# Lists and router bias in bf16 terms, and tokens' weights stored in eight runs

## The chip, the cores and the metric

One NeuronCore of a Trainium2 chip runs the whole kernel. The metric is the device time of one execution in microseconds (us), taken as the median of several runs. Engines are named as in the profile: PE (TensorE, with its weight loads as PEld), DVE (VectorE), ACT (ScalarE), POOL (GpSimd) and SP (SyncE); SP, ACT and POOL also issue DMAs.

## The reference, cut to what matters

A graph layer is followed by a mixture of experts. 1024 nodes (tokens) have 512 features, there are 16384 edges sorted by destination, and 64 experts of which each token takes 2.

```python
HW = layernorm(x) @ W
x1 = x + relu(segment_sum(edge_val[:, None] * HW[edge_col], edge_row) + bias)
xt = layernorm(x1)
scores = sigmoid(xt @ Wg.T + bg)              # 1024 x 64
w, idx = top_k(scores, 2);  w = w / w.sum(-1, keepdims=True)
nx = layernorm(xt)
h1 = einsum('td,edh->eth', nx, gamma * W1) + b1 + beta @ W1
h3 = einsum('td,edh->eth', nx, gamma * W3) + b3 + beta @ W3
y  = einsum('eth,ehd->td', silu(h1) * h3 * cw, W2) + cw @ b2   # cw: w at the two chosen experts
z  = a small shared expert of 32 hidden units
out = x1 + y + z
```

The kernel computes each expert only for the tokens that chose it. All inputs and outputs are fp32.

## The kernel before, in words

P is 128. The 1024 tokens are NT = 8 tiles of 128 rows. The order of the work on each engine is written out by hand (`manual_schedule`): every engine runs its instructions in program order, and semaphores hold it where data is missing.

**Graph part.** The sorted edges are cut into 128 x 2 windows of destinations. For each of 16 groups `one_hots` builds selection matrices (DVE, ACT), `matrix_group` multiplies them on PE into a dense weighted adjacency, `turn` transposes it, and `weighted_sum` multiplies it with `hws`, the transformed features (tile `acc`, L514). In the second round of eight groups, at g = 6, `bias_terms` splits the experts' biases b1 and b3 into three bf16 terms each, whose sum gives the fp32 value; this splitting on DVE already exists before the change.

**Tile loop (L686).** Iteration t runs a pipeline over the tiles, whose steps share the engines:
- `weighted_sum` of tile t on PE, in three portions; between them stand `turn`, `listed(t - 3)`, `score_bias(t - 1)`, `turn_x(t - 1)`, `rank(t - 2)` and, last, `scores(t - 1)`.
- `finish(t)` on DVE: bias, relu, residual, statistics of the layer norm, normalized row (`res`, `bnst`, `mvr`, L529 to L541). `summed` loads the row's base from DRAM through POOL's queue.
- `store_nx(t - 1)`: ACT scales the row (L545), POOL stores it to `nx_d` in DRAM, from where experts' rows are gathered.
- `score_bias` (L558) opens the accumulation of the router's scores with a matmul of a row of ones with `brow`, the router's bias `bg` followed by zeros; `scores` (L563) adds the product with `wall`.
- `choose` (DVE) takes the best two experts; `rank` (PE, L597 and L599, bf16) counts how many earlier tokens chose the same expert; `put` (DVE) turns that into a slot (`here`, L611).
- `slots` (L614) builds two one-hot matrices for each of the two choices: `so` (L620), token by slot, and `bo` (L622), token by pair of experts, multiplied with the entry's number `numb`, 2 x token + choice - PAD with PAD = 16384. It runs on POOL, for the last tile on DVE. `listed` (L628) adds so^T bo into the PSUM tile `plist`, two fp32 matmuls for a tile. A profile shows each fp32 matmul of this kind as two instructions.

At the end `plist` plus PAD gives `lists` (L719), the entry numbers by pair of experts, 64 rows for each expert, and `tokens` (L720), half of them.

**Expert part (L1008).** 33 blocks are walked in `order`: 32 pairs of experts of up to 64 tokens each, and one block for experts with more than 64. For block n: `fetch` gathers token rows from `nx_d` (POOL, L752), `front` transposes and scales them (`scaled`: PE, DVE), `hidden` multiplies with W1 and W3 (L781) and applies Silu (ACT, L784), `turned` transposes (L793), `outputs` multiplies with W2 (L803) and copies to `xy` (ACT, L806), `scatter` writes the rows to `y_d` (POOL, L810). `load_until` has SP issue the expert weights, 512 KB a transfer, up to AHEAD = 13 experts ahead into a ring of tiles; a transfer waits until the tile's former reader on PE is done. `weights` (L826) divides the two best scores by their sum and stores them, 2048 numbers, to `w_d` in DRAM; it stands after the first block's `hidden`. The last blocks' weights are gathered from `w_d` by `block_weights`. `beyond`, at block 6, makes the lists for the experts with more than 64 tokens, with fp32 one-hot matrices of its own and `numb`. ACT fills the three gather buffers `rows_of` with zeros before the first gathers (L1010).

## Time and profile before

| what | value |
|---|---|
| median of 3 runs | 447.22 us (446.52 to 449.56) |
| the profiled execution's own time | 446.42 us |
| its span, first to last instruction | 444.7 us |
| PE / PEld busy | 391.5 us (88%) / 185.0 us (42%) |
| DVE / ACT / POOL busy | 243.8 / 117.2 / 122.0 us |
| DMA | 132.50 MB, mean 298 GB/s |
| mean granted TensorE clock | 0.966 |

Durations come from the one profiled execution. A busy PE is not PE at its peak, since matmuls are pipelined and their ends are modelled; the distance between two starts is the better measure of what an instruction holds PE for. The chain that ended last follows the last instruction back from releaser to releaser. A wait is put down to the semaphore that came last. In the timeline a matmul's bracket gives the idle time of the engine before it and what ended it. Names in the profile leave out buffer numbers: `ph<-brow,ones` is `score_bias`, `plist<-bo,so` is `listed`, `acc<-hw,AT` is `weighted_sum`, `pt<-ident,row` is `turn_x`, `pt<-ident,A` is `turn`.

### The profile page before, as it was taken

How to read it: one execution, taken by the hardware profiler on the slowest of the kernel's cores; microseconds unless marked ns; L12 is line 12 of the kernel's file. 1: busy time of each engine (PE TensorE's matmuls, PEld its weight loads, DVE VectorE, ACT ScalarE, POOL GpSimd, SP SyncE). 2: the span in 40 equal slices, each digit the busy share in tenths (PEclk: the TensorE clock that was granted, in tenths of full speed). 3: DMA queues.
4: the chain of work that ended last, by engine and by line, in shares of the span. 5: the costliest groups of instructions: out<-in, count | busy, mean ns of one | idle time of the engine just before them, and what ended most of it. 6: DMA issues, size and time to landing. Idle time of an engine off the chain costs nothing.

```text
span 444.7 us, 6426 instructions
## 1 busy us (share of the span) xinstructions
PE 391.5 (88%) x2130; PEld 185.0 (42%) x2130; DVE 243.8 (55%) x723; ACT 117.2 (26%) x241; POOL 122.0 (27%) x162
## 2 busy tenths in 40 slices
PE   2999769988999953799967999999999999999693
PEld 1554446644655542343422444343443443433141
DVE  4869899658777783423275444443424323421791
ACT  1235799332231130121101221212221221212100
POOL 5450800003333343223232232322322331303100
PEclk9999999999999975899998999999999999999898
DMA  8367392991723397379999999999999999998572
GB/s 255 105 109 107 127 359 104 408 370 67 255 70 127 123 407 285 134 248 412 409 407 407 407 409 405 409 408 408 406 408 407 409 407 406 406 407 343 193 298 89
DMA packets 40983, 132.50 MB, mean 298 GB/s; under 512 B 7116, under 2 KB 7260, under 8 KB 40816
## 3 DMA queue, kind: packets, MB, share of 16 engines
q1 hardware_dynamic: 31040, 109.66, 63.2%
q0 software_dynamic: 9184, 20.28, 14.9%
q10 hardware_dynamic: 720, 2.10, 1.2%
q8 instruction: 18, 0.29, 0.3%
q14 instruction: 21, 0.17, 0.1%
HBM read 124.13 MB, written 18.62 MB: 321 GB/s over the span
## 4 chain that ended last, share of the span: by engine, by line
PE 59%; DMA 13%; DVE 9%; ACT 5%; issue 2%; POOL 0%; POOLq 0%; ACTq 0%; DVEq 0%
PE xph L781 18%; PE acc L514 11%; DMA y_d<-xy,lists 10%; PE xpy L803 9%; PE xpt L193 3%; ACT ov L417 2%; PE ph L495 2%; PE xpht L793 2%; PE xph L777 2%; PE pt L507 1%; PE ph L563 1%; DMA y_d<-xy,lists_o 1%; PE xpy L942 1%; ACT A L500 1%; PE xpy L909 1%
## 5 line engine op out<-in xcount | busy, mean ns | idle before, releaser
L781 PE MATMUL xph<-w,xT 128*64 128x512 f32 (+1 forms) x520 | 122.5, 600 | 0.1
L810 POOL DMA_INDIRECT y_d<-xy,lists x30 | 31.1, 1037 | 145.3 <-ACT xy L806 53.7
L803 PE MATMUL xpy<-w,xhT 128*64 128x512 f32 (+1 forms) x260 | 66.0, 610 | 4.7 <-ACT xhT L795 4.7
L781 PEld LDWEIGHTS xph<-w,xT 128*64 128x64 f32 (+1 forms) x520 | 38.7, 139 | 62.2 <-issue 58.4
L786 DVE TENSOR_TENSOR xh<-xa,xph 128x256 f32<-128x256 f32 x33 | 13.9, 420 | 87.7 <-ACT xa L784 87.7
L514 PE MATMUL acc<-hw,AT 128*128 128x512 f32 x128 | 60.7, 600 | 0.4 <-ACT AT L508 0.4
L784 ACT ACTIVATE xa<-xph 128x256 f32<-128x256 f32 x33 | 12.6, 383 | 114.1 <-PE xph L781 114.1
L752 POOL DMA_INDIRECT rows<-nx_d,tokens x32 | 34.7, 1083 | 17.2 <-issue 7.3
L803 PEld LDWEIGHTS xpy<-w,xhT 128*64 128x64 f32 (+1 forms) x260 | 19.4, 141 | 45.0 <-issue 39.4
L764 DVE TENSOR_TENSOR xT<-xpt,gT 128x512 f32<-128x512 f32 x32 | 22.1, 689 | 26.5 <-PE xpt L193 26.2
L806 ACT COPY xy<-xpy 128x512 f32<-128x512 f32 x33 | 19.3, 585 | 49.8 <-PE xpy L803 44.1
L307 PE MATMUL ph<-w_sb,hT 128*128 128x512 f32 x64 | 31.2, 636 | 0.7 <-ACT hT L300 0.7
L514 PEld LDWEIGHTS acc<-hw,AT 128*128 128x128 f32 x128 | 22.1, 191 | 17.3 <-issue 16.7
L193 PE MATMUL xpt<-ident,rows 128*128 128x128 f32 x132 | 22.0, 293 | 5.9 <-DMA rows<-nx_d,tokens 5.9
L546 POOL DMA_DIRECT2D nx_d<-row x8 | 4.5, 560 | 73.8 <-ACT row L545 73.8
L417 ACT CAST ov<-eq 128x1536 f32<-128x1536 bf16 x16 | 24.7, 1552 | 0.0
L766 DVE TENSOR_TENSOR xT<-xT,bT 128x512 f32<-128x512 f32 x32 | 22.2, 693 | 1.1
L495 PE MATMUL ph<-ov,ol 128*32 128x128 f32 x512 | 17.4, 276 | 5.4 <-ACT A L500 5.0
L193 PEld LDWEIGHTS xpt<-ident,rows 128*128 128x128 f32 x132 | 19.3, 211 | 6.0 <-DMA rows<-nx_d,tokens 6.0
L793 PEld LDWEIGHTS xpht<-ident,xh 128*128 128x128 f32 x66 | 11.8, 212 | 20.8 <-DVE xh L786 12.7
L793 PE MATMUL xpht<-ident,xh 128*128 128x128 f32 x66 | 15.1, 311 | 6.0 <-DVE xh L786 6.0
L193 PE MATMUL pt<-ident,row 128*128 128x128 f32 x64 | 11.6, 306 | 8.4 <-DVE row L187 2.8
(271 smaller groups left out, 503.9 us busy)
## 6 DMA issues: line engine op xcount, KB each, us to landing
w<-in_L_ffn_W_dram SPq DMA_DIRECT2D x195, 512.0 KB, 11.1
y_d<-row POOLq DMA_DIRECT2D x1, 4096.0 KB, 14.5
ys<-y_d SPq DMA_DIRECT2D x8, 512.0 KB, 7.8
base_d<-in_L_gnn_bias_dram POOLq DMA_DIRECT2D x1, 2048.0 KB
row<-base_d POOLq DMA_DIRECT2D x8, 256.0 KB, 3.2
nx_d<-row POOLq DMA_DIRECT2D x8, 256.0 KB, 3.6
w_sb<-in_L_gnn_W_dram ACTq DMA_DIRECT2D x1, 1024.0 KB, 5.3
res<-in_x_dram SPq DMA_DIRECT2D x2, 512.0 KB, 10.6
```

The costliest lines, as they stand in the source:

```text
L193: nc.tensor.transpose(ps[:, k, :], v[:, k, :], ident[:n, :n])
L307: nc.tensor.matmul(ph, hT[:, k, :], w_sb[:, k, :], start=(k == 0), stop=(k == KC - 1))
L417: nc.scalar.copy(ov[:, :, :VA], eq)
L495: nc.tensor.matmul(pa[LO * w:LO * (w + 1), u, :], ol[:, q, :], ov[:, q, :], start=True, stop=True)
L514: nc.tensor.matmul(accs[t], ATs[h][t // 4][:, t % 4, wq, :], hws[h][:, wq, :], start=(h == 0 and wq == 0), stop=(h == NH - 1 and wq == NQ ...
L752: nc.gpsimd.indirect_dma_start(out=rows, out_offset=None, in_=nx_d[:, :], in_offset=bass.IndirectOffsetOnAxis(ap=of, axis=0), bounds_check ...
L764: nc.vector.tensor_tensor(xT.rearrange(view, n=n), pt.rearrange(view, n=n), g[:, :, :, None].to_broadcast(over), ALU.mult)
L766: nc.vector.tensor_tensor(xT.rearrange(view, n=n), xT.rearrange(view, n=n), b[:, :, :, None].to_broadcast(over), ALU.add)
L781: nc.tensor.matmul(ph[n * r:(n + 1) * r], xT[:, k, n * r:(n + 1) * r], w13[:, :, k, :], start=False, stop=(k == KC - 1))
L793: nc.tensor.transpose(pt[:, c, :], v[:, c, :], ident)
L803: nc.tensor.matmul(py[n * r:(n + 1) * r], hT[:, c, n * r:(n + 1) * r], w2[:, c, :], start=(c == 0), stop=(c == HC - 1))
L810: nc.gpsimd.indirect_dma_start(out=y_d[:, :], out_offset=bass.IndirectOffsetOnAxis(ap=numbers, axis=0), in_=y, in_offset=None, bounds_chec ...
```

## The change

- `slots` builds `so` and `bo` in bf16. Each entry number is split into two terms, the tile's base 256 t - 16384 and 2 x partition + choice (`near`, a new iota), so `bo` has two halves and one more instruction for each choice; `listed` adds four bf16 matmuls for a tile.
- `brow` becomes 65 rows, with `bg` loaded into rows 0, 32 and 64; at g = 6 a loop takes the three bf16 terms of the bias into those rows of `brow3`, and `score_bias` is one bf16 matmul with K = 65.
- `weights` transposes the two columns of weights on PE, copies them on ACT into an eight-row tile, and stores eight runs of 256 numbers.
- `weights` moves ahead of `front(0)`, behind the first three gathers.
- An activation with Silu on one column of `found` is added behind the filling of `rows_of`.

```diff
--- before.py
+++ after.py
@@ -230,6 +230,9 @@
             nc.gpsimd.iota(diff, pattern=[[1, P]], base=0, channel_multiplier=-1, allow_small_or_imprecise_dtypes=True)
             nc.gpsimd.iota(numb, pattern=[[2 * P, NT], [1, 2]], base=-PAD, channel_multiplier=2,
                            allow_small_or_imprecise_dtypes=True)
+
+            near = gp.tile([P, 2], F32, name="near")
+            nc.gpsimd.iota(near, pattern=[[1, 2]], base=0, channel_multiplier=2, allow_small_or_imprecise_dtypes=True)
             nc.gpsimd.iota(partid, pattern=[[0, 1]], base=0, channel_multiplier=1, allow_small_or_imprecise_dtypes=True)
             nc.gpsimd.iota(tile_at, pattern=[[P, NT]], base=0, channel_multiplier=0, allow_small_or_imprecise_dtypes=True)
             at_i = gp.tile([P, P], I32, name="at_i")
@@ -252,8 +255,12 @@
             nc.vector.tensor_scalar(win[:, 1:2], win[:, 0:1], float(P), None, op0=ALU.add)
             nc.vector.tensor_scalar(thr, win, float(DL), None, op0=ALU.mult)
             nc.vector.tensor_scalar(before_b, diff, 0.0, None, op0=ALU.is_gt)
-            brow = gp.tile([1, P], F32, name="brow")
+
+            BR = 65
+            brow = gp.tile([BR, P], F32, name="brow")
             nc.vector.memset(brow, 0.0)
+            brow3 = gp.tile([BR, P], BF16, name="brow3")
+            nc.vector.memset(brow3, 0.0)
 
 
 
@@ -343,7 +350,8 @@
             bs13 = gp.tile([1, 2 * HS], F32, name="bs13")
             nc.gpsimd.dma_start(bs13[:, :HS], bs1[None, :])
             nc.gpsimd.dma_start(bs13[:, HS:], bs3[None, :])
-            nc.gpsimd.dma_start(brow[:, :E], bg[None, :])
+            for n in range(3):
+                nc.gpsimd.dma_start(brow[32 * n:32 * n + 1, :E], bg[None, :])
             b13 = mid([3 * EH, 2, 2, H], "b13", F32)
             for n in range(3):
                 for a in range(2):
@@ -555,7 +563,7 @@
 
             def score_bias(t):
                 pls[t] = psh.tile([P, D], F32, name="ph")[:, :P]
-                nc.tensor.matmul(pls[t], ones[0:1, :], brow, start=True, stop=False)
+                nc.tensor.matmul(pls[t], ones_b[:BR, :], brow3, start=True, stop=False)
 
             def scores(t):
                 pl = pls.pop(t)
@@ -616,16 +624,20 @@
                 here = ohots.pop(t)
                 ohots[t] = []
                 for n in range(2):
-                    so = rt.tile([P, P], F32, name="so", bufs=4)
+                    so = rt.tile([P, P], BF16, name="so", bufs=4)
                     engine.tensor_scalar(so, rank_at, here[:, n:n + 1], None, op0=ALU.is_equal)
-                    bo = rt.tile([P, NP], F32, name="bo", bufs=4)
-                    engine.tensor_scalar(bo, iota[:, :NP], pair[:, t, n:n + 1], numb[:, t, n:n + 1],
+                    bo = rt.tile([P, 2, NP], BF16, name="bo", bufs=4)
+                    engine.tensor_scalar(bo[:, 0, :], iota[:, :NP], pair[:, t, n:n + 1], float(2 * P * t - PAD),
+                                         op0=ALU.is_equal, op1=ALU.mult)
+                    engine.tensor_scalar(bo[:, 1, :], iota[:, :NP], pair[:, t, n:n + 1], near[:, n:n + 1],
                                          op0=ALU.is_equal, op1=ALU.mult)
                     ohots[t].append((so, bo))
 
             def listed(t):
                 for n, (so, bo) in enumerate(ohots.pop(t)):
-                    nc.tensor.matmul(plist, so, bo, start=(t == 0 and n == 0), stop=(t == NT - 1 and n == 1))
+                    for m in range(2):
+                        nc.tensor.matmul(plist, so, bo[:, m, :], start=(t == 0 and n == 0 and m == 0),
+                                         stop=(t == NT - 1 and n == 1 and m == 1))
 
             As = [[big([P, P // NS, DL, HI // 2], "A") for n in range(2)]]
             for g in range(8):
@@ -659,6 +671,12 @@
                 matrix_group(As[1], 1, g, ohs.pop(0))
                 if g == 6:
                     bias_terms()
+                    for n in range(3):
+                        term = gp.tile([BR, P], BF16, name="term")
+                        nc.vector.tensor_copy(term, brow)
+                        nc.vector.tensor_copy(brow3[32 * n:32 * n + 1, :], term[32 * n:32 * n + 1, :])
+                        if n < 2:
+                            nc.vector.tensor_sub(brow, brow, term)
                 turn(As[0], 0, g)
                 if g:
                     n0, n1 = len(ahead) * (g - 1) // 7, len(ahead) * g // 7
@@ -828,7 +846,13 @@
         nc.vector.reciprocal(wts[:, :, 0], wts[:, :, 0])
         nc.vector.tensor_mul(wts[:, :, 1], top[:, :, 1], wts[:, :, 0])
         nc.vector.tensor_mul(wts[:, :, 0], top[:, :, 0], wts[:, :, 0])
-        nc.gpsimd.dma_start(w_d.rearrange("(i p n) o -> p i (n o)", p=P, n=2), wts)
+
+        pt = psx.tile([P, D], F32, name="xpy")
+        for n in range(2):
+            nc.tensor.transpose(pt[:NT, n * P:(n + 1) * P], wts[:, :, n], ident)
+        wT = bp.tile([P, D], F32, name="xy", bufs=2)[:NT, :2 * P].rearrange("i (p n) -> i p n", n=2)
+        nc.scalar.copy(wT.rearrange("i p n -> i n p"), pt[:NT, :2 * P].rearrange("i (n p) -> i n p", n=2))
+        nc.gpsimd.dma_start(w_d.rearrange("(i r) o -> i (r o)", i=NT), wT.rearrange("i p n -> i (p n)"))
 
         nc.vector.tensor_mul(rs2, vs[:, :, 0], rs[:, :, 0])
         nc.vector.tensor_mul(rs2, rs2, rs[:, :, 1])
@@ -1008,8 +1032,11 @@
     with tc.manual_schedule(engines={ENG.PE, ENG.DVE, ENG.Activation, ENG.Pool, ENG.SP}):
         for rows in rows_of:
             nc.scalar.activation(rows, ones[:, 0:1].to_broadcast([P, D]), AF.Copy, scale=0.0)
+
+        nc.scalar.activation(found[:, 0:1], ones[:, 0:1], AF.Silu)
         for n in range(NR):
             fetch(n)
+        weights()
         front(0)
         fetch(NR)
         front(1)
@@ -1040,8 +1067,6 @@
                 back(n - 1)
             else:
                 y_last = [outputs(*hTs.pop(LAST - 1))]
-            if n == 0:
-                weights()
             if n == BEYOND:
                 beyond()
             if 2 <= n - BEYOND < 2 + NT:
```

## The prediction

> **What bounds the kernel now.** I read the chain that ended last first, then the same chain in windows, then the timeline of each join, then the waits of SP's queue and the table of windows. The page's chain names the engines:
>
> ```profile
> PE 59%; DMA 13%; DVE 9%; ACT 5%; issue 2%; POOL 0%; POOLq 0%; ACTq 0%; DVEq 0%
> ```
>
> In order of time: up to 106 us DVE, ACT and PE alternate; from 106 to 155.6 us, the tile loop, every piece is PE's; to 178 us it is one long chain of small steps for the last tile, ending in the list and the first gather; from 178 us the experts run, PE's pieces to 346 us and then the scatters. One tile of the loop, in the chain (start, us, what):
>
> ```profile
> 107.95 3.44 PE acc L514 x8
> 111.39 0.45 PE pt L507 x4
> 111.83 0.37 PE plist L628 x4
> 112.20 1.80 PE acc L514 x4
> 114.00 0.41 PE ph L558 x2
> 114.41 0.68 PE pt L193 x4
> 115.09 0.03 PE ph L597
> 115.12 0.03 PE ph L599
> ```
>
> The reader is to see that the list (L628) and the router's bias (L558), both fp32, lie on PE's path in each tile, and that two bf16 matmuls of 64 columns (L597, L599) move it by 0.03 us each. A tile takes 9.88 us.
>
> **The experts.** Three resources are nearly level there. PE is busy 103.16 of 104 us between 241 and 345 us. SP's queue waits for room behind its own transfers (53.2, 47.8 and 46.8 us at L740, L734, L733 after 170 us) at 407 GB/s, and PE waits for a weight only at 401.7 us (0.7). Scatters wait for the one before from 350 us on. So a start that is earlier moves all three; a cheaper block in the middle would not.
>
> **The change, part by part.** Saved time is positive.
>
> *Bias, L558.* An fp32 matmul of K = 1 is two instructions; the new one is a single bf16 instruction of K = 65, 128 columns. The price is read from the starts: the four acc instructions before it start 0.43 apart from 112.03, so PE is free at 113.75, yet L558 starts at 113.93, and the transposes after it at 114.34. The bias thus takes 0.59 us of PE, of which its own columns explain 2 x 0.107 (as a 128-column fp32 transpose takes 0.107 in its group); the rest is gap on both sides. Lower bound of the new cost: twice L597's 64 columns, 0.06; upper: the same gaps remain and only one pass of columns goes, 0.43. I take 0.12, near the bf16 row, since the fp32 128-row matmuls show no such gaps. Saves 0.47 (0.16 to 0.53). On the path for tiles 2 to 6, five times: 2.35 (0.8 to 2.65). For tiles 0, 1 and 7 PE waits for DVE's row afterwards (2.1, 1.1 and 2.78 us idle): nothing.
>
> *List, L628.* Two fp32 matmuls (four instructions, 0.36 from start to start) become four bf16 instructions on twice the products. [...] The row: L597 and L599, with the same 128x128 bf16 weights, move PE by 0.03 each, so four cost 0.12 and a tile saves 0.24. [...] I take 0.20: saves 0.16 (-0.07 to 0.24), five times on the path: 0.8 (-0.35 to 1.2).
>
> PE reaches the rank (L597) 0.63 earlier per tile then. It now arrives 0.8 us after DVE's chosen (113.99 against 114.81), so 0.2 of cover is left; and DVE is idle 0.72 before each finish at 116.98. DVE is next in line but not yet late. If it is late by more, half of these 3.15 us stay.
>
> *Last tile.* Here the extra work lies on the path. Rank(7) stands on PE behind listed(6), which waits for POOL (timeline: start us, us, engine, line, operation, count, idle time before and its releaser):
>
> ```profile
> 165.78 0.47 POOL L622 TENSOR_SCALAR bo<-iota,pair,numb 128x32 f32<-128x32 f32 x1
> 166.30 0.50 PEld L628 LDWEIGHTS plist<-bo,so 128*128 128x128 f32 x2 [0.54 <-POOL bo L622]
> 166.75 0.24 PE L597 MATMUL ph<-chosen,before_b 128*128 128x64 bf16 x1
> 167.08 0.29 DVE L605 TENSOR_TENSOR tmp<-oh,ph 128x128 f32<-128x128 bf16 x1
> ```
>
> POOL gets two more bo instructions; bo to next so is 0.45 us, so it ends 0.9 later, and after it PE has one bf16 matmul instead of two fp32 instructions that took 0.45 here (166.30 to 166.75). Rank(7) is 0.6 later, and DVE's tmp, which has no slack (L592 ends as it starts), 0.57. Then DVE makes slots(7) itself, six instructions instead of four at 0.2 each: 0.4. Against it, after DVE's last bo only one short matmul follows instead of most of the four fp32 ones: from 169.16 to the lists at 169.92 are 0.76, then some 0.3. Sum: 0.57 + 0.4 - 0.46 = 0.5 lost (0 to 1.3; the upper end if each bo costs POOL 0.8, between its 0.47 and its slowest, 0.96). Earlier tiles have 2 us between POOL's last bo and listed, an iteration later, so 0.9 is covered; base loads, queued behind slots on POOL, are issued at 110.07 for use at 116.98 and land in 3.2: also covered.
>
> *Silu first.* At the first block ACT stands in PE's way:
>
> ```profile
> 184.02 1.28 ACT L784 ACT_TABLE_LOAD   x1 [17.43 <-PE xph L781]
> 185.31 0.38 ACT L784 ACTIVATE xa<-xph 128x256 f32<-128x256 f32 x1
> 186.21 0.50 PE L793 MATMUL xpht<-ident,xh 128*128 128x128 f32 x2 [2.26 <-DVE xh L786]
> 187.17 0.96 POOL L831 DMA_DIRECT2D w_d<-wts  x1 [7.68 <-DVE rs L834]
> ```
>
> PE waits 2.26 us through it. The added activation on one column pulls the load to about 167 us, into ACT's 17.43 idle us, with copies alone before the next Silu (copies between Silus load nothing now). Saves 1.28. [...] If Silu's set were dropped again, it saves 0.
>
> *Weights moved.* Six DVE instructions of 0.17 (1.1 us) now run from 170.3, two PE transposes (below 0.5) and an ACT copy (0.4) follow: done by about 172.7. All lie beside the first gather, issued at 171.22 on tokens that exist already and landing at 175.75. On POOL the store comes after three gathers, at 175.3, for 0.55 to 0.96, before fetch(3), which waits until 177.19 for PE's transposes. SP is passed nowhere. DVE's and ACT's queues hold nothing else until 176.96. Cost nothing; without that cover 2 us.
>
> *The store itself.* Before, 1024 pieces of 8 bytes; after, eight of 1 KB. This stands beside it now (window: us, busy PE, PEld, DVE, ACT, POOL, clock, DMA share, GB/s):
>
> ```profile
> 190.00:192.00 2.00, 2.00 (x12) 0.64 (x10) 0.42 (x1) 0.38 (x1) 0.00 (x0) 1.00 0.82 303
> 192.00:194.00 2.00, 2.00 (x14) 1.11 (x12) 0.36 (x1) 0.86 (x2) 0.32 (x1) 1.00 0.38 68
> 194.00:196.00 2.00, 2.00 (x12) 0.64 (x10) 1.02 (x2) 0.00 (x0) 1.69 (x2) 1.00 0.49 80
> 198.00:200.00 2.00, 2.00 (x14) 1.00 (x12) 0.28 (x1) 0.83 (x2) 0.00 (x0) 1.00 1.02 411
> ```
>
> Loads issued at 191 us hardly move for 4 us: about 3.3 us of the full rate are lost. Most of it should come back to DMA, which then no longer ends the last blocks; PE's two short waits near 401 and 408 us (0.7, 0.6) and a slow last scatter can shrink. As PE and the scatters are nearly as late, I count 0.3 (0 to 2).
>
> *Early parts.* One iota (0.14 to 0.22), larger memsets (0.17), two more bias loads on POOL (0.5 each, before POOL's 15.43 us wait at 44.10), and eight DVE instructions of some 0.2 at g = 6: DVE ends at 85.2 and is then idle 6.80 us until 92.01. Nothing; if that cover were gone, 1.8.
>
> **Sum.** 2.35 + 0.8 - 0.5 + 1.28 + 0.3 = 4.2 us. The profiled execution took 446.42 (span 444.7), giving 442.2. The median shown, 447.22, is 0.8 above it; I forecast 442.7 for a median, a little nearer to the profile because 449.56 pulls the three runs up.
>
> **Rivals.**
> [...]
> 2. *Experts pinned by DMA.* If the last weight rather than PE's start sets the end, the 1.28 is absorbed and only the loop's 2.65 remain: 444.5. For it: 407 GB/s throughout. Against: the lost 3.3 us come back to this very queue.
> 3. *DMA was the real bound.* Then the store's removal gives 2 us more: 440.5. Against: the scatters chain from 350 us.
> 4. *The loop turns to DVE, or the gaps around the bias remain.* About half of 3.15 stays: 444.3.
>
> **Numbers.** Forecast 0.44, rivals 0.09, 0.17, 0.14, 0.16. One per cent, about what a measurement of this kernel can tell, is 4.5 us, so the forecast lies on that line: half of it and rival 3 and a little more are faster (0.41), rivals 2 and 4 and the other half no change (0.50), rival 1 slower (0.09). The range, 439.8 to 446.8, takes in rivals 2 to 4 and the ends of the costs (bias -1.5, list -1.1, last tile -0.8).
>
> **To be seen after.** L558 one instruction, transposes at most 0.2 us after it starts; the tile pitch 9.25 instead of 9.88; POOL's last bo and rank(7) 0.6 later against here(6); no table load at the first L784; the dip of 68 to 80 GB/s gone. A pitch of 9.8, or a wait of listed for POOL in the loop, proves me wrong.

## The result and the profile after

The changed kernel takes 440.8 us (median of 4 runs, 440.67 to 442.39) beside 447.2 of the kernel before (four runs as well). The ratio is 0.988 (95% interval 0.984 to 0.993), which is 5.2 us less (3.4 to 7.1); the two medians differ by 6.4. The profiled execution took 440.67, its span is 438.9; before, 446.42 and 444.7.

The changed kernel's page, the chain that ended last by engine:

```profile
PE 62%; DMA 10%; DVE 9%; ACT 4%; issue 2%; POOL 0%; POOLq 0%; ACTq 0%; DVEq 0%
```

PE's share of the path has grown from 59% to 62% though its work shrank: what went was waiting on DMA and ACT. One tile of the loop in the changed kernel's chain (start, us, what). L522 was L514, L515 L507, L639 L628, L566 L558, L605 and L607 L597 and L599, L571 L563:

```profile
118.20 3.44 PE acc L522 x8
121.64 0.45 PE pt L515 x4
122.09 0.09 PE plist L639 x4
122.18 1.81 PE acc L522 x4
123.99 0.06 PE ph L566
124.05 0.53 PE pt L193 x4
124.58 0.03 PE ph L605
124.61 0.03 PE ph L607
```

The bias holds PE for 0.06 us, the list's four instructions for 0.09. The next tile starts at 127.32, so the pitch is 9.12 instead of 9.88, and there is still no wait for DVE or POOL in it.

Where ACT met the first block (timeline of the changed kernel: start, us, engine, line, operation; the bracket is idle time before and its releaser):

```profile
169.24 1.28 ACT L1036 ACT_TABLE_LOAD   x1
170.54 0.20 ACT L1036 ACTIVATE found<-ones 128x1 f32<-128x1 f32 x1
170.65 0.36 ACT L854 COPY xy<-xpy 8x256 f32<-8x256 f32 x1
180.33 0.38 ACT L802 ACTIVATE xa<-xph 128x256 f32<-128x256 f32 x1 [9.32 <-PE xph L799]
```

The load has gone into ACT's idle time, and L802 follows PE at once. The store's dip is gone as well (table of windows, changed kernel: window, us, busy PE, PEld, DVE, ACT, POOL, clock, DMA share, GB/s):

```profile
190.00:192.00 2.00, 2.00 (x12) 0.70 (x10) 0.07 (x1) 0.00 (x0) 1.01 (x1) 1.00 0.94 293
192.00:194.00 2.00, 2.00 (x10) 0.42 (x6) 0.42 (x1) 0.39 (x1) 0.00 (x0) 1.00 0.97 374
194.00:196.00 2.00, 2.00 (x14) 1.25 (x14) 0.91 (x2) 0.86 (x2) 0.00 (x0) 1.00 1.03 414
```

That much went as the forecast had it. To see the rest, I cut each trace at the same instructions: the first `acc` of tile 2, the first `acc` of tile 7, the `lists`, the first W1/W3 product of the second block, the ninth of the 16 W1/W3 products of the 31st block (its middle, 1.72 us behind its first in every trace), and the end of the span. The stretches in us, each from starts in the trace, with the experiments below beside them:

| kernel | to tile 2 | to tile 7 | to lists | to 2nd block | to mid-31st block | to the end | span |
|---|---|---|---|---|---|---|---|
| before | 91.81 | 55.08 | 23.03 | 17.44 | 208.82 | 48.48 | 444.7 |
| changed | 91.27 | 53.87 | 22.61 | 14.63 | 208.79 | 47.73 | 438.9 |
| e1 bias only | 91.48 | 54.73 | 22.84 | 14.39 | 208.84 | 45.00 | 437.3 |
| e2 lists only | 91.86 | 56.92 | 22.91 | 15.61 | 209.04 | 45.44 | 441.8 |
| e3 Silu only | 91.70 | 55.08 | 23.04 | 14.24 | 208.90 | 45.49 | 438.5 |
| e4 weights only | 90.80 | 56.74 | 23.31 | 14.39 | 208.82 | 46.74 | 440.8 |
| e5 changed again | 91.05 | 53.85 | 22.62 | 14.46 | 208.80 | 47.56 | 438.3 |
| e6 warm early | 91.61 | 52.20 | 22.62 | 15.86 | 207.21 | 46.75 | 436.2 |
| e9 tail's order | 91.95 | 55.09 | 22.65 | 14.92 | 208.81 | 45.34 | 438.8 |
| e10 warm and order | 90.96 | 52.21 | 23.09 | 13.87 | 209.99 | 43.91 | 434.0 |
| e12 changed, old store | 91.64 | 52.20 | 22.57 | 14.09 | 209.23 | 44.40 | 434.1 |

Each trace is one run. Those of e3 and e12 are of their fastest run (440.2 where the median is 444.1, 435.9 where it is 438.5), those of e2, e4 and e9 of their slowest. So the stretches tell where time goes, and the medians below how much.

Two things stand out in the first two rows. The stretch to tile 7 gained 1.21 us, though four pitches became shorter (three by 0.76, the last, which has no `turn`, by 0.58: 2.87 in all). And the first 91 us and the end gained 0.54 and 0.75 without an edit that explains it. The windows of the two kernels at tiles 2 and 3 say what happened, first the changed kernel's:

```profile
102.40:105.80 3.40, 1.33 (x8) 0.89 (x7) 2.99 (x18) 1.36 (x3) 0.54 (x1) 1.00 0.01 5
105.80:109.20 3.40, 3.40 (x11) 2.38 (x10) 2.98 (x9) 0.33 (x2) 2.13 (x4) 0.51 0.22 81
109.20:112.60 3.40, 3.40 (x11) 1.57 (x10) 2.91 (x18) 0.00 (x0) 1.63 (x4) 0.99 0.27 73
```

then the kernel before:

```profile
103.70:107.10 3.40, 1.89 (x9) 1.28 (x10) 3.05 (x18) 1.34 (x2) 0.54 (x1) 1.00 0.12 39
107.10:110.50 3.40, 3.40 (x15) 1.97 (x14) 3.13 (x12) 0.33 (x2) 3.00 (x5) 1.00 0.12 43
```

PEclk, the third figure from the right, is 0.51 in the changed kernel for one window after PE was busy 1.33 of 3.40 us, and 1.00 in the kernel before after 1.89 of 3.40. At half clock scores(0) and tile 3's first products took 1.66 us longer than before. In all traces the half-clock stretches, except the one that runs into a trace's end (5.1 us before, 4.0 in the changed kernel), are whole multiples of 3.41 us (3.4, 6.8, 17.1, 20.5), on a grid whose offset from the program's start differs from run to run (1.24 us before, 0.03 in the changed kernel).

### The profile page after: what moved, and what is told of

It is laid out like the page before. It is cut to its first block, busy times and chain, and to the rows that moved or that the text cites. A ratio compares the mean times of both kernels' runs of the same rounds, so it can differ in the third digit from the quotient of the medians.

```text
span 438.9 us, 6445 instructions
## 1 busy us (share of the span) xinstructions
PE 387.6 (88%) x2124; PEld 181.5 (41%) x2124; DVE 245.1 (56%) x734; ACT 117.8 (27%) x243; POOL 130.0 (30%) x179
## 4 chain that ended last, share of the span: by engine, by line
PE 62%; DMA 10%; DVE 9%; ACT 4%; issue 2%; POOL 0%; POOLq 0%; ACTq 0%; DVEq 0%
PE xph L799 20%; PE acc L522 12%; PE xpy L821 10%; DMA y_d<-xy,lists 7%; PE xpt L193 3%; ACT ov L425 2%; PE xpht L811 2%; PE xph L795 2%; PE ph L503 2%; PE ph L571 2%; PE pt L515 2%; PE xpy L966 1%; DMA y_d<-xy,lists_o 1%; ACT A L508 1%; PE xpy L933 1%
## 5 line engine op out<-in xcount | busy, mean ns | idle before, releaser
L799 PE MATMUL xph<-w,xT 128*64 128x512 f32 (+1 forms) x520 | 120.6, 599 | 0.2 <-DVE xT L784 0.2
L821 PE MATMUL xpy<-w,xhT 128*64 128x512 f32 (+1 forms) x260 | 64.6, 612 | 3.2 <-ACT xhT L813 3.2
L522 PE MATMUL acc<-hw,AT 128*128 128x512 f32 x128 | 61.5, 608 | 0.4 <-ACT AT L516 0.4
L802 ACT ACTIVATE xa<-xph 128x256 f32<-128x256 f32 x33 | 12.7, 385 | 120.7 <-PE xph L799 120.7
L522 PEld LDWEIGHTS acc<-hw,AT 128*128 128x128 f32 x128 | 22.3, 193 | 17.5 <-issue 16.9
```

The costliest lines, as they stand in the source:

```text
L522: nc.tensor.matmul(accs[t], ATs[h][t // 4][:, t % 4, wq, :], hws[h][:, wq, :], start=(h == 0 and wq == 0), stop=(h == NH - 1 and wq == NQ ...
L799: nc.tensor.matmul(ph[n * r:(n + 1) * r], xT[:, k, n * r:(n + 1) * r], w13[:, :, k, :], start=False, stop=(k == KC - 1))
L821: nc.tensor.matmul(py[n * r:(n + 1) * r], hT[:, c, n * r:(n + 1) * r], w2[:, c, :], start=(c == 0), stop=(c == HC - 1))
```

## The experiments

All are timed against the kernel before on the same chip, whose runs lie between 444.0 and 450.2 us there, with medians of 445.9 to 447.0.

**One part at a time (e1 to e4).** Each is the kernel before with one part of the change.

e1:

```diff
-                nc.tensor.matmul(pls[t], ones[0:1, :], brow, start=True, stop=False)
+                nc.tensor.matmul(pls[t], ones_b[:BR, :], brow3, start=True, stop=False)
```

with the loads and the splitting of `brow3`.

> The kernel before with only the router's bias as one bf16 matmul of K = 65. Theory A (the four parts lie on paths of their own and add up): the bias goes from 0.59 to 0.06 us per tile, five tiles, so the tile loop's pitch falls from 9.88 to about 9.35 and the end moves by -2.0 to -2.65 us. Theory B (the experts are pinned by their weights' DMA, not by when PE starts): the loop ends 2.65 earlier, but under half of it reaches the end: -0.5 to -1.3. Theory C (PE arriving earlier at the rank then waits for DVE's choice): pitch 9.6, end -1.3. A and C are told apart by PE's wait ahead of the rank, A and B by the stretch from the first gather to the end. If the drop of the granted clock at 105 to 109 us, which the changed kernel shows and the one before does not, comes from this part, scores(0) takes 1.7 instead of 0.9 us here and 1.7 us of it are lost again.

e2: `so`, `bo` and `near` as in the change, and

```diff
-                    nc.tensor.matmul(plist, so, bo, start=(t == 0 and n == 0), stop=(t == NT - 1 and n == 1))
+                    for m in range(2):
+                        nc.tensor.matmul(plist, so, bo[:, m, :], start=(t == 0 and n == 0 and m == 0),
+                                         stop=(t == NT - 1 and n == 1 and m == 1))
```

> The kernel before with only so and bo in bf16 and four list matmuls per tile. Theory A (parts add up; the four bf16 instructions cost 0.10 us instead of 0.36): pitch 9.88 to about 9.62, five times 0.26 = -1.3, last tile about +0.15 by POOL's longer work, so -1.1 us at the end (-0.6 to -1.5). Theory B (weight loads of 128 columns cost the same in bf16): pitch unchanged or +0.07, end +0.15 to +0.9. Theory D (last tile loses the 0.5 of the prediction, since here the half clock of the last tile starts later than in the changed kernel): end -0.8, and rank(7) 0.6 later against here(6). If this part brings the clock drop at 105 to 109 us, the end is +0.6 later than before.

e3:

```diff
+        nc.scalar.activation(found[:, 0:1], ones[:, 0:1], AF.Silu)
         for n in range(NR):
             fetch(n)
```

> The kernel before with only one more activation with Silu on one column, ahead of the first gathers. Theory A: the table load of 1.28 us leaves the path of the first block and PE's start of the second block is 1.28 to 1.33 earlier; since everything behind starts earlier, the end moves by the same: -1.0 to -1.4 us. Theory B (experts pinned by DMA, whose transfers wait for room and not for this): PE starts 1.3 earlier and waits for weights later, end 0 to -0.3. Theory E (Silu's tables are dropped again before the first block): load still there, 0.

e4: `weights` with transposes and eight runs, and

```diff
+        weights()
         front(0)
...
-            if n == 0:
-                weights()
```

> The kernel before with only the weights turned and stored in eight runs ahead of the first front. Theory A (the DMA dip beside the store, 68 to 80 GB/s for 4 us, was covered by weights loaded ahead): dip gone, end within 0.3 us of the kernel before. Theory F (the lost 3.3 us of DMA came back as late last weights or scatters): dip gone, end -0.7 to -2, with PE's waits near 401 and 408 us and the last scatters shorter. Theory G (the store in the old place also held ACT, POOL or DVE at the first block): first block 0.3 to 0.5 earlier. A loss of 0.5 to 2 would mean that the six DVE instructions or the transposes stand in the way of the first block's front.

| kernel | median us | range, runs | ratio to before, 95% interval |
|---|---|---|---|
| e1 bias only | 438.9 | 438.4 to 439.7, 6 | 0.985 (0.981 to 0.989) |
| e2 lists only | 441.2 | 439.7 to 443.5, 6 | 0.989 (0.985 to 0.993) |
| e3 Silu only | 444.1 | 440.2 to 446.3, 22 | 0.994 (0.992 to 0.996) |
| e4 weights only | 441.0 | 438.6 to 442.6, 6 | 0.989 (0.984 to 0.993) |

Taken as differences of medians, the four parts gain 8.0, 5.6, 2.7 and 5.8 us, 22 in all (by the ratios 19.5), where the whole change gains 6.4 and, run again, 4.8 (by the ratios 5.2 and 5.1). No theory expected that. The traces separate it. In the loop the parts do add: e1's pitch is 9.38 (-0.50), e2's 9.63 (-0.25), together the 0.76 of the changed kernel. What comes on top has three sources that are not the part itself:

1. *Silu's table load* left the path in e1, e2 and e4 too, which have no added activation. e1's timeline of ACT:

```profile
167.10 1.28 ACT L795 ACT_TABLE_LOAD   x1 [1.21 <-DVE here L615]
181.32 0.38 ACT L795 ACTIVATE xa<-xph 128x256 f32<-128x256 f32 x1 [12.94 <-PE xph L792]
```

The load belongs to the first L795, but here it runs ahead of that instruction's wait for PE, in the kernel before and in e11 (below) behind it. Why these two have it on the wrong side I can't say; that it is worth 1.3 us only once, whichever part brings it, is read from the rows.

2. *The clock's grid.* e1, e2 and e4 lost 1.7 to 2.9 us between tiles 2 and 4 by half-clock windows (e2 two, e1 and e4 one), the kernel before and e3 none. In the first block it went the other way: half clock lasted until 3.7 us after its first W1/W3 product in the kernel before, 1.8 in the changed one, 0.8 to 2.5 in e1 to e4.

3. *The end.* From the middle of the 31st block it took 45.0 to 45.5 us in e1, e2 and e3 and 46.7 in e4, but 48.5 before and 47.7 in the changed kernel. This is larger than any part, and e9 and e12 are about it.

Of e3's theories A names the cause and is too small in the time: in its trace, that of its fastest run, the second block starts 3.3 us earlier, of which the load is 1.28 and the clock in that block 1.4, and the median is 2.7 lower. PE then waited for weights in the last blocks: 7.53 us from the middle of the 31st block's products to the middle of the 32nd's, as in e1 (7.39), where the kernel before took 6.88.

**The changed kernel again (e5).** No edit.

> The changed kernel once more, for its spread and for a second sample of where the half-clock stretches fall. Theory P (the TensorE clock is granted in free-running windows of 3.41 us, and a window after one in which PE was busy under about half is granted half; the windows' phase against the program is chance): the time varies from run to run by 2 to 5 us with the mean granted clock, as the kernel before varied from 444.2 to 449.3; the trace's half-clock stretches are whole multiples of 3.41 us, and each follows a window with PE under about 0.52 busy. Theory Q (the clock falls at fixed places of the program, by its power or its kind of work): the same stretches at the same places as in the first trace, 105.8, 157.0, 221.9, 232.1, 409.6 and 436.9 us. Median 439.5 to 442.5.

Median 441.2 (438.5 to 442.7, 6 runs), ratio 0.989 (0.985 to 0.992). This grid happened to lie within 0.6 us of the first trace's, and the half-clock stretches lie at the same places, so this run alone doesn't tell P from Q. One is missing, that of 221.9 us, after a window with PE 0.46 busy in both traces. The runs' mean clock goes from 0.966 to 0.951, and the three slowest have the lowest.

Over all traces of this study (that of before included) it went so: from full clock, a window with PE busy under 0.42 was followed by half clock in every case, one over 0.56 never, and between these it went either way (half after 0.46 at 218.5 us in the changed kernel, full after 0.48 at 229.9 us before); from half clock, full clock came back after windows of 0.95 and more, and never under 0.92. These busy shares are those of matmuls with modelled ends.

**PE kept busy early (e6).** The changed kernel, and in `plist`'s bank, on columns that nobody reads:

```diff
+            def keep_warm(n):
+                for _ in range(n):
+                    nc.tensor.matmul(plist_bank[:, D // 2:], ones_b[:3 * EH, :], bias3[:, 0, :D // 2],
+                                     start=True, stop=True, skip_group_check=True)
...
                     score_bias(t - 1)
+                    keep_warm({1: 18, 2: 12}.get(t, 0))
```

> The changed kernel with 18 and 12 added bf16 matmuls (96 rows, 256 columns, results unused) on PE where it waits for DVE in tiles 0 and 1 (between score_bias and the transposes). Theory P: the windows between 96 and 106 us are over half busy then, no half clock falls on 105 to 109 us, and scores(0) and the first products of tile 3 keep 0.9 and 3.44 us: -1.0 to -1.7 us against the changed kernel where its window fell there. Theory Q: the half clock stays, and the added matmuls cost 0 to +1 us. Theory R (the added matmuls stand in PE's way when DVE's row comes): +0.5 to +2 us, whatever the clock.

Median 437.8 (437.5 to 439.3), ratio 0.982 (0.980 to 0.984). In its trace PE is busy 2.65 us of the window from 103.5 to 106.9, where the changed kernel had 1.33, the next window has the full clock, and the stretch to tile 7 takes 52.20 instead of 53.87. This trace alone doesn't tell P from Q, though: e12, which has no added matmuls, fell on the same grid (offset 1.08 us in both), and there 1.85 us in that window were enough as well (52.20). What decides is a pair whose grids lie within 0.08 us: e5, the changed kernel, and e10 (below), which has these added matmuls too. First e5's windows, then e10's (columns as above):

```profile
101.90:105.30 3.40, 1.33 (x8) 0.72 (x7) 2.98 (x18) 1.63 (x3) 0.36 (x1) 1.00 0.00 0
105.30:108.70 3.40, 3.40 (x12) 2.37 (x12) 2.62 (x11) 0.00 (x0) 2.05 (x4) 0.50 0.23 81
```

```profile
101.90:105.30 3.40, 2.65 (x20) 1.93 (x19) 2.99 (x17) 1.55 (x3) 0.44 (x1) 1.00 0.00 0
105.30:108.70 3.40, 3.40 (x15) 1.96 (x15) 3.16 (x11) 0.33 (x2) 2.05 (x5) 1.00 0.20 77
```

In the same window PE is busy 1.33 us and half clock follows, or 2.65 us and full clock follows; the stretch to tile 7 takes 53.85 in the one and 52.21 in the other. Of the four traces with the early matmuls (e6, e7, e8, e10) none has half clock between tiles 2 and 4; of the ten without, six have it, and the other four are those with offsets of 1.03 to 1.24 us. In this pair work that nobody needs made the work behind it faster, so the clock followed PE's idleness, and the time followed the clock: P, not Q. Against the 441.2 of e5, on the same chip, the median of e6 gains 3.3, more than the 1.67; in this trace another 1.6 came from a half-clock window less at 232 us, far behind the added matmuls.

**PE kept busy late (e7, e8).** e7 adds matmuls before the lists of tiles 5 to 7, after score_bias(7) and after the weights' transposes; e8 also 34 before the last block's wait. The late ones open a new sum in the bank that holds `plist`, and the output of these two kernels is off by 0.24; so only what lies ahead of the lists is read.

> As before, and added matmuls in the chain of the last tile too: 18, 12 and 16 ahead of the lists of tiles 5, 6 and 7, 16 after score_bias(7), 34 after the transposes of the weights. Theory P: the 17 to 20 us of half clock from 157 us, most of which PE spends waiting, shrink to at most one or two windows; turn_x(7) and scores(7) 0.4 us shorter, the first block's transposes and W1/W3 products about 1.5 to 3 us shorter: -2 to -4 us against the kernel with early ones alone. Theory Q: half clock stays, 0 to +1. Theory R (PE comes late to rank(7), to the lists or to the first front by its own added work): +0.5 to +3 us.

> As before, and 34 added matmuls after the products of the last block but one, where PE waits about 3 us for the last gathers (410 to 414 us). Theory P: no half clock between 405 and 425 us; the last block and what follows run at full clock: -1.5 to -3 us against the kernel without these, where its window fell there, and a spread of the runs under 1.5 us. Theory Q: 0. Theory R: the added matmuls delay the last block's first products by up to 1 us.

Times 433.3 and 436.4 us, not comparable. In e7 the half clock that began at 157.0 us in the changed kernel and lasted 20.5 does not begin before 173.0 (after a window with PE 0.43 busy) and lasts 6.8, and in e8 it lasts one window, 173.2 to 176.6: the long stretch is dissolved too. Whether the matmuls at the end of e8 help is left open.

**The tail's order (e9).** The changed kernel with one line moved:

```diff
-                hots_last = [block_hots(tokens[:, NP - 2 + m:NP - 1 + m], w_last[m]) for m in range(2)]
...
             h = hidden(xTs.pop(n), parts)
+            if n == LAST:
+                hots_last = [block_hots(tokens[:, NP - 2 + m:NP - 1 + m], w_last[m]) for m in range(2)]
```

> The changed kernel with one line moved: the two one-hot matrices of the last blocks (bhots) are built on DVE behind the last block's product xh, not ahead of it. Theory S (the end hangs on the chain scatter, weights' gather bw, bhots, xh: in the changed kernel xh of the last block stands on DVE behind bhots until 411.3 us, while PE waits 3.8 to 5 us, and that wait does not move with what PE saves earlier): the wait ahead of the last xpht shrinks from about 4 us to under 0.7, no half clock falls on the last products, the time falls by 3 to 6 us against the changed kernel. Theory T (PE's work and the scatters set the end, and DVE's order there is covered): within 0.5 us. Theory U (the block's sums then wait for bhots instead, and the outputs' order keeps its end): -1 to -2 us.

What it is about, in the changed kernel's chain:

```profile
396.34 5.78 DMA y_d<-xy,lists
...
402.20 0.60 ACT xy L824
...
402.88 0.99 POOL y_d L828
403.87 0.11 POOL bw L972
...
404.25 2.31 DMA bw<-w_d,lists
...
406.65 2.16 DVE bhots L984 x8
...
409.18 2.13 DVE bhots L984 x8
411.31 0.34 DVE xh L804
```

The gather of the last blocks' weights (`bw`) stands on POOL behind a scatter, which stands behind the scatter before (the copy on ACT between the two holds nothing up, see e12); the one-hot matrices need `bw`; and the last block's xh, which needs neither, stands behind them on DVE. PE waits for it (timeline of PE, changed kernel):

```profile
405.22 1.88 PE L821 MATMUL xpy<-w,xhT 128*64 128x512 f32 x8
411.70 0.70 PE L811 MATMUL xpht<-ident,xh 128*128 128x128 f32 x2 [4.59 <-DVE xh L804]
```

In e9 xh runs at 408.11, right behind PE's products (407.64), the wait of 4.6 is gone and no half clock falls on the last products. The median is 438.3 (434.9 to 440.5), ratio 0.979 (0.975 to 0.983), 2.5 and 2.9 us under the two medians of the changed kernel (4 by the ratios); the stretch to the end is 45.34 instead of 47.73, in e9's slowest run. S names the wait rightly, and the size lies between U's and the lower half of S's: PE then waits 2.0 us for the rows `ys`, which are read back after the last scatter.

**Both (e10).** e9's line, e6's matmuls and e7's late ones, of which those in the bank of `plist` now accumulate (start=False) so that the lists keep their entries, with 44 after the weights' transposes.

> The changed kernel with the moved line of the tail, and with added matmuls as in the kernel with early and late ones (the late ones now accumulate onto unused columns instead of starting anew, so that the lists are kept; 44 instead of 34 after the weights' transposes). If Theory P (windows of 3.41 us, half clock after a window under half busy) and Theory S (the chain over bhots) both hold, the gains add: no or at most one half-clock window between 100 and 180 us, the first block's products at full clock, and the tail without its wait: 430 to 434 us, -7 to -11 against the changed kernel. If the granted clock were only a sign of load and not a cause (Theory Q): equal to the tail's gain alone. If the experts are pinned by the scatters' chain, what is won before 180 us is lost by 400 us and only the tail's gain remains, 435 to 437.

Median 435.1 (434.4 to 437.4), ratio 0.974 (0.970 to 0.978). One half-clock window is left between 100 and 180 us (e10's windows):

```profile
163.40:166.80 3.40, 3.40 (x22) 2.44 (x20) 2.26 (x13) 1.22 (x3) 0.00 (x0) 0.50 1.02 412
166.80:170.20 3.40, 3.40 (x33) 3.02 (x31) 0.00 (x0) 1.93 (x3) 2.16 (x2) 1.00 0.96 363
170.20:173.60 3.40, 2.91 (x23) 2.13 (x21) 0.72 (x2) 0.39 (x1) 1.70 (x3) 1.00 0.27 79
173.60:177.00 3.40, 2.68 (x13) 1.38 (x15) 1.96 (x3) 0.00 (x0) 1.91 (x2) 1.00 0.28 76
```

From the first block's first W1/W3 product to the second's it takes 5.81 us, in the changed kernel 6.66. This version is 12 us under the kernel before and about 6 under the changed one. That is the sum of what e6 (3.3) and e9 (2.5 to 2.9) gained one by one, 1 us short of what P and S expected with the late matmuls, and at the edge of the last theory's range, 435 to 437. So the late matmuls show no gain of their own in the time: the stretch to the middle of the 31st block is 209.99, 1.2 longer than in the changed kernel, with two half-clock windows from 228.2 us. How much of that is the grid and how much the scatters' chain is open.

**What was expensive in the bias (e11).** The kernel before with the fp32 bias over 65 rows, 64 of them zero:

```diff
-                nc.tensor.matmul(pls[t], ones[0:1, :], brow, start=True, stop=False)
+                nc.tensor.matmul(pls[t], ones[:BR, :], brow, start=True, stop=False)
```

> The kernel before with the bias's fp32 matmul over K = 65 rows (rows 1 to 64 of brow are zeros) instead of K = 1; what is computed is the same. Theory V (the 0.38 us of gaps around the bias, beyond its columns, come from fp32 as such): the bias keeps about 0.59 us per tile, pitch 9.88. Theory W (they come from the change of K, from 128 rows to one and back): pitch about 9.5, as fp32 instructions of 128 rows show no such gaps. One look: the pitch between the starts of tiles 4, 5 and 6 and the start of the transposes after the bias tell, not the total.

Its chain in the loop:

```profile
121.48 1.80 PE acc L516 x4
123.28 0.22 PE ph L560 x2
123.50 0.48 PE pt L193 x4
```

The same two fp32 instructions now take 0.22 us and nothing is lost around them; the pitch is 9.49. So W, in one trace: of the 0.53 that the bias gained, 0.37 come from K = 1 against K = 65, and 0.16 from one bf16 pass instead of two in fp32. (One run, 442.1 us.)

**The store alone undone (e12).** The changed kernel with the old `weights` in its old place: the form of the store and its place are both taken back and not told apart.

> The changed kernel with the weights' store left as before: 2048 numbers in pieces of 8 bytes, behind the first block. Bias, lists and Silu are as in the changed kernel. Theory B (rival 2 of the prediction: the last weights' DMA pins the experts once PE starts earlier): the dip of DMA at 186 to 194 us is back, PE waits for weights in the last two blocks, and from the start of block 30's products to the end of the last block's takes 15.5 to 17.5 us instead of 14.2; if nothing covers that, the time is 1.3 to 3 us above the changed kernel's 441.0. Theory S (the last block's xh stands behind bhots on DVE anyway): PE's wait for weights is there, but PE's wait ahead of the last xpht is shorter by as much, and the time is within 0.7 us of the changed kernel. Theory G (the store in the old place holds POOL or ACT at the first block too): block 1 starts 0.3 to 0.5 later against block 0.

The dip is back (188 and 125 GB/s from 186 to 190 us), and the stretch from the middle of the 31st block's products (not from their start, as the expectation has it) to the end of the last W1/W3 product takes 16.1 us instead of 14.2: B's wait for weights is there. Yet the median is 438.5 (435.9 to 438.8), ratio 0.981 (0.976 to 0.986): 2.3 and 2.7 us *below* the two medians of the changed kernel, with intervals that just overlap. S has the right wait, but not the size, within 0.7. e12's chain at the end (of its fastest run):

```profile
395.30 8.23 DMA w<-in_L_ffn_W_dram
403.53 2.14 DVE bhots L978 x8
...
406.04 2.14 DVE bhots L978 x8
408.19 0.34 DVE xh L804
```

and its PE:

```profile
408.57 0.51 PE L811 MATMUL xpht<-ident,xh 128*128 128x128 f32 x2 [1.01 <-DVE xh L804]
```

`bw` had been issued at 398.27, 3.9 us after the 32nd block's first W1/W3 product, against 404.25, 8.4 after it, in the changed kernel. (It landed at 403.44, just ahead of `bhots`, so the load of weights in the chain's first line stands for it.) That is a matter of the scatters. Each waits for the one before: from its landing to the next one's start 0.75 to 0.80 us pass in nearly every block, in e12 as in the changed kernel, with a copy on ACT between them or without. Where nothing else holds them, they mostly start 6.6 to 7.0 us apart in the changed kernel, and a block mostly takes PE 6.4 to 7.4 there. In e12 a late scatter starts 2 to 3.5 us after its copy `xy`; in the changed kernel 4 to 8. In all traces with the whole change this lag begins at one and the same scatter, the 23rd, which starts 9.0 to 9.5 us after the 22nd where e12 has 6.9, though the one before had landed at 349.9 and its own copy was done at 347.6 in the changed kernel. The same scatter in the changed kernel's and in e12's timeline of POOL:

```profile
353.04 1.04 POOL L828 DMA_INDIRECT y_d<-xy,lists  x1 [6.93 <-ACT xa L802]
```

```profile
349.08 1.03 POOL L828 DMA_INDIRECT y_d<-xy,lists  x1 [4.54 <-DMA y_d<-xy,lists]
```

The releaser named in the first line came late by chance. The records of POOL's sequencer show the hold: in the changed kernel the semaphore's record ahead of the 23rd scatter ends at 349.93, 0.04 behind the landing, and the next record, a MOVE, starts 2.89 us later, where 0.51 is usual. So long the sequencer stands still there in all seven traces with the whole change. In the kernel before, e2, e3 and e11 it stands still for 2.70 us ahead of the 20th scatter; in e1, e4 and e12 nowhere between the 16th and the 30th. So the old store with one load of `bg` has it, the old store with three loads has not, the new store with one load has not, and the new store with three has it again: it goes with neither the store's form nor the number of loads alone. What the sequencer does in that time the traces don't show. From the 23rd scatter to the 30th the lag is 1.9 to 4.2 us without the standstill and 3.7 to 7.8 with it; yet e2 and e3 have it and an early end, so it is only a part of what makes the end late.

## Why the prediction came out as it did

The forecast was 442.7 us with 439.8 to 446.8; measured 440.8 and, again, 441.2. Against the profile it had 4.2 us; the traces show 5.8. The range held, and so did the main mechanism, the bias and the list on PE's path and Silu's load; by its steps, in us saved:

| step | predicted | traces |
|---|---|---|
| bias and list in the loop | 3.15 | 3.4 (2.9 in four pitches, 0.55 in tile 7's own step) |
| last tile | -0.5 | -0.1 |
| Silu's load | 1.28 | 1.3 |
| store and the end | 0.3 | 0.75 (all of the end) |
| clock at tiles 2 and 3 | not seen | -1.7 |
| clock in the first block | not seen | 1.0 |
| first gather, its landing | not seen | 0.6 |
| first 91 us | 0 | 0.5 |

- *Bias.* Taken as 0.12, measured 0.06. The reading that the rest of the 0.59 was gaps was right; e11, with 0.22 for the same two fp32 instructions over 65 rows, shows that they belong to K = 1 and not to fp32. The 0.107 of a 128-column fp32 transpose fits the bias's own two instructions, which start 0.213 apart before; L507's transposes mostly start 0.109 to 0.115 apart there.
- *List.* 0.36 to 0.09: 0.27 saved instead of 0.16, just beyond the upper end that the rows of L597 and L599 gave (0.24). The 0.20 that the forecast took for the four, and its lower end, a loss of 0.07, were the author's estimate, and no run shows them. A single load's record at L639 is 0.10 us long, but lengths may not be added here: the four weight loads of 128 bf16 columns and their products start 0.025 to 0.03 us apart and hold PE for 0.09.
- *Pitch.* 9.25 forecast, 9.12 measured. Rival 4 (DVE takes over, or gaps stay) is out.
- *Last tile.* The step "Rank(7) is 0.6 later" was half right: against here(6) it is 0.34 later (2.95 before, 3.29 after, both from start to start; e2 has the same). POOL's bo instructions took 0.39 and 0.47, so its part ends 0.8 later, but from the last bo to rank(7) are now 0.1 us instead of 0.5. In this pair even that is hidden, because half clock made turn_x(7) 0.38 longer (1.13 against 0.75) and so the scores later; e6 and e12, with full clock there, have rank(7) 0.35 and 0.32 later against the scores. After it the lists come 0.2 earlier. The six DVE instructions of the weights did not run from 170.3, either: they stand among choose(7)'s at 163.5 to 165.0 in DVE's gaps, so the written order does not hold across the border between the tile loop and the expert part. Rival 1, a slower kernel, is out.
- *Silu.* The size is exact in the pair of traces. What the prediction could not know is that the load's place was an accident of the kernel before: e1, e2 and e4 have it early without the added line. The figure of 1.28 us from the trace held: the load is as long at its new place, 169.24 us.
- *Store.* "Most of it should come back to DMA" is right: PE's wait for weights in the last blocks went (14.2 against 16.1 us). The next clause, that the scatters are "nearly as late", was weighed too lightly: the scatters' lag, `bw` and bhots end the last block, and in the kernel before the scatters lag from the 20th on, at 336.5 us, not from 350. That the store gains 0.3 is not borne out: with the old store the whole change is 2.3 to 2.7 us faster (e12), while the new store alone goes with a gain (e4). POOL's standstill comes and goes between these kernels, so the store's own share is not known. Rival 2's wait is there without the store's change, 1.9 us, but covered by one on DVE; the 2 us that rival 3 expected from the store did not come.
- *The clock.* Missing as a term. The prediction used the mean granted clock nowhere, although the profile of before has digits of 7 and 5 in its PEclk row for the last tile. PE need not be idle for half clock to follow: in the changed kernel 0.39 of a window of 3.41 us busy was too little. The clock's terms (-1.7, 1.0 and the 0.5 of the first 91 us) nearly cancelled in this pair; that the total came out this near the forecast is in that part luck.

## What to carry to other kernels

- Look for half-clock windows in the row of the granted clock before pricing a change on PE: here the window behind one of 3.41 us with PE less than about half busy (0.42 to 0.56) had half the clock, so a saving just ahead of a wait can be lost on the work behind it, and unused matmuls in the wait can win it back.
- One part timed alone is not its share of the whole. By the medians four parts gained 22 us one by one and 5 to 6 together, because an accident of instruction order, the clock's grid and the tail's lag came with each; compare stretches of the traces, not totals.
- Before an engine gets a long preparation (here 4.6 us of one-hots on DVE), ask what short instruction of the critical chain stands behind it in its queue. Moving one line was worth 2.5 to 2.9 us, nearly as much as the loop's whole saving.

## What the hardware showed unexpectedly

- The clock's grid starts anywhere against the program. Its offset (the start of a half-clock stretch modulo 3.41 us) orders even the first 46 us: from 0.03 to 2.53 us of offset the last L307 product ends later and later, 46.2 (changed), 46.4 (e1), 46.6 (e3), 46.75 (before), 46.9 (e2), 47.0 (e9), 47.4 (e8), and at 2.71 it falls back to 45.7 (e4). All fourteen traces are in this order to within 0.1 us. The profile's first record of the clock, a full one, is at 12.95 us in e4 and at 16.18 in e8, 3.2 us later, and the first eight L307 products take 5.1 us in e4 and 6.7 in e8; what the clock was ahead of that record is not shown. The 0.5 us of the first 91 us go with this order (tile 2 starts at 90.80 in e4 and at 92.45 in e8); how much of the spread of 444 to 450 us for one kernel goes with it is not shown.
- A K = 1 fp32 matmul of 128 columns cost 0.59 us between others of K = 128 in the kernel before; over 65 rows, with zeros, 0.22 in e11.
- A scatter of 128 rows took 5.8 to 7.6 us to land while weights streamed at 407 GB/s (before and changed kernel), about as long as a block of PE's work (mostly 6.4 to 7.4); here their chain was a third bound beside PE and the loads.
- POOL's sequencer stood still for 2.89 or 2.70 us ahead of one fixed scatter, in eleven of the fourteen traces; with two more small loads or another form of one store it came ahead of another scatter or of none.
